# A relational graph layer: when a finished node tile is weighted, and in how many steps the next layer's front follows

## The chip, the core and the metric

The kernel runs on one core of one Trainium2 chip. Its time is the device time of one execution in microseconds (us); lower is better. TensorE (PE in the profile, with its weight loads as PEld) multiplies, VectorE (DVE) and ScalarE (ACT) do elementwise work and copies, GpSimd (POOL) issues gathers by software, and SyncE (SP) issues plain transfers. Each engine takes its instructions in program order.

## The reference

The model is a stack of four layers on a graph of 3125 nodes with 256 features and 50,000 edges. Each layer is a graph part and a feed-forward part, both added to the node features `x`. The change lies in the last layer's graph part, and in what opens the feed-forward part behind it:

```python
def _L3_gnn_ref(node_repr, weight, bias, edge_index, edge_types):
    h_all = jnp.einsum('ni,roi->rno', node_repr, weight)      # 8 relations
    src, dst = (edge_index[0], edge_index[1])
    msgs = h_all[edge_types, src]
    messages = jax.ops.segment_sum(msgs, dst, num_segments=node_repr.shape[0])
    return messages + bias

x = x + _L3_gnn_ref(_layernorm(x), ...)
x = x + _L3_ffn_ref(_layernorm(x), ...)   # 8 experts, the best one of each node, softmax(x @ gate_w + gate_b)
```

Each edge has one of 8 types (relations). A node receives the sum, over its incoming edges, of the source's normalised features times the matrix of the edge's type. The feed-forward part normalises `x` again, computes logits of 8 experts per node, and sends each node through its best expert, of limited capacity.

## The kernel before

The graph part sums first and multiplies afterwards: for every node and every relation the source features are summed over the edges of that type, and only the sums are multiplied by the relation's matrix. Edges are sorted by destination by an earlier stage. `l3_gnn` walks over them in 196 **quarters** of 256 edges, 16 destination nodes to a quarter on average; a node tile of 128 nodes is 8 quarters. One turn of the loop, quarter q:

- Two gathers by POOL (line 681), each of 128 edges' source rows, into the tile `g`. The rows are bf16 and hold three parts of 256 whose sum is the fp32 value, so a gather brings 196 KB. `g` has 12 buffers, one to a quarter.
- Two one-hot matrices `hot` on DVE (line 1703): 128 edges by 192 places (8 relations x 24 nodes).
- 12 bf16 matmuls on PE (line 1708): transposed features times one-hot into the PSUM tile `sum`, which has 4 buffers.
- DVE reads the quarter's place in the ring (line 1712) and adds `sum` to the running sums `acc` (line 1714). `acc` is a ring of 512 nodes plus a margin of 24.
- `weighted(1, q)`: one relation of the oldest tile that was taken out at least two quarters ago: two fp32 matmuls, which the trace shows as 4 rows (line 1685), from the copy `done` into the PSUM tile `po`.
- When the tile's last quarter has passed (`last[t] == q`), `finished(t)`: ACT copies the tile's sums to `done` (line 1664, two buffers) and clears them in `acc` (line 1665); for every fourth tile, where the ring wraps, the margin is added and cleared as well (lines 1669 and 1670).

After the eighth relation DVE adds `po` to `x` (line 1689), and `then` is called: `l3_ffn_front(t)`. It makes the layer norm of the tile (lines 529 to 534, on DVE with a square root on ACT), issues three transfers of 128 KB on SP (lines 1733, 1734 and 1737: the normalised tile, `x` for later, and `x` as the output so far), transposes the normalised tile on PE (two matmuls, `f_tr`, line 1740), copies that out of PSUM on ACT (`f_xT`, line 1742), multiplies by the gate's weights on PE (`f_mm`, line 563), and adds the gate's bias on DVE (`pr`, line 1745). `po` has two PSUM buffers, `f_tr` and `f_mm` one each.

The order of an engine's work is settled ahead of the run by a scheduler, from the order of the program and its estimates; waits between engines are semaphores. `tc.issue_after(i)` holds what is issued inside it behind instruction i on the engine of i. Before the change PE's order at the end of a tile is: a po row of the next tile's first relation, the two f_tr, the other po row, one sum of the next quarter, the two f_mm, the remaining eleven sums (rows here are matmuls as the program has them, two to a relation). For 185 sums no po comes at all; then one relation comes with each quarter. After the last sums 36 po rows follow, with the f_tr and f_mm of three tiles between and behind them.

The stage behind, `l3_ffn`, begins with the softmax of the logits on DVE and the experts' weight transfers on SP (line 1804), directly after this stage's end.

A second version of the graph part (`l3_gnn_of_any`) stands in the other branch of a test on the data; it does not run here.

Of the kernel before, what the change touches and what calls it, by code (L numbers as in the profile page):

```python
# [22 lines left out]
P = 128  # L23
# [4 lines left out]
D = 256  # L28
# [24 lines left out]
NQ = -(-E // QE)  # L53
# [10 lines left out]
def rows_of(t):  # L64
    return P if t < NT - 1 else TAIL
# [3 lines left out]
def gnn_ffn_stack(ctx: ExitStack, tc: tile.TileContext, a: dict, out: bass.AP):  # L69

    nc = tc.nc
# [890 lines left out]
    with ExitStack() as s:  # L962
        pp = s.enter_context(tc.tile_pool(reuse_waits="tile", name="l0_ps", bufs=2, space=PSUM))
# [3 lines left out]
        wp = s.enter_context(tc.tile_pool(reuse_waits="tile", name="l0f_w", bufs=2))  # L967
# [29 lines left out]
    with ExitStack() as s:  # L997
        sp = s.enter_context(tc.tile_pool(reuse_waits="tile", name="cells_s", bufs=1))
        bp = s.enter_context(tc.tile_pool(reuse_waits="tile", name="cells_x", bufs=2))
        pp = s.enter_context(tc.tile_pool(reuse_waits="tile", name="cells_ps", bufs=2, space=PSUM))  # L1000
# [132 lines left out]
    with tc.If(nc.values_load(slow_path[0:1, 0:1], min_val=0, max_val=1) > 0) as any_order:  # L1133
        with ExitStack() as s:
            ep = s.enter_context(tc.tile_pool(reuse_waits="tile", name="any_e", bufs=1))
            gp = s.enter_context(tc.tile_pool(reuse_waits="tile", name="any_w", bufs=3))
            pp = s.enter_context(tc.tile_pool(reuse_waits="tile", name="any_ps", bufs=2, space=PSUM))
            adj1 = build_graph_of_any(ep, gp, pp)
        with ExitStack() as s:
            lp = s.enter_context(tc.tile_pool(reuse_waits="tile", name="l1a", bufs=1))  # L1140
            wp = s.enter_context(tc.tile_pool(reuse_waits="tile", name="l1a_w", bufs=2))
            ap = s.enter_context(tc.tile_pool(reuse_waits="tile", name="l1a_adj", bufs=1))
            pp = s.enter_context(tc.tile_pool(reuse_waits="tile", name="l1a_ps", bufs=1, space=PSUM))
            l1_gnn_of_any(lp, wp, ap, pp, adj1)
    with any_order.Else():
        with ExitStack() as s:
            lp = s.enter_context(tc.tile_pool(reuse_waits="tile", name="l1g", bufs=1))
            wp = s.enter_context(tc.tile_pool(reuse_waits="tile", name="l1g_w", bufs=3))
            pp = s.enter_context(tc.tile_pool(reuse_waits="tile", name="l1g_ps", bufs=2, space=PSUM))
# [170 lines left out]
    with ExitStack() as s:  # L1320
        pp = s.enter_context(tc.tile_pool(reuse_waits="tile", name="l1f_ps", bufs=2, space=PSUM))
# [107 lines left out]
    with ExitStack() as s:  # L1429
        lp = s.enter_context(tc.tile_pool(reuse_waits="tile", name="l2g", bufs=1))  # L1430
        wp = s.enter_context(tc.tile_pool(reuse_waits="tile", name="l2g_w", bufs=2))
        ap = s.enter_context(tc.tile_pool(reuse_waits="tile", name="l2g_adj", bufs=3))
        pp = s.enter_context(tc.tile_pool(reuse_waits="tile", name="l2g_ps", bufs=2, space=PSUM))
# [180 lines left out]
    def l3_gnn_of_any(lp, wp, pp, wT, then):  # L1614

        rel = dram.tile([NP * NR, D], F32, name="rel")
        acc = lp.tile([P, NT, D], F32, name="acc")
        nc.vector.memset(acc, 0.0)
        xT = lp.tile([P, KC, NP], F32, name="xT")
        for t in range(0, NT, SG):  # L1620
            parts = wp.tile([P, SG, 3 * D], BF16, name="l3_in")
            nc.sync.dma_start(parts, tab_3[t * P : (t + SG) * P, :].rearrange("(t p) c -> p t c", p=P))
            z = wp.tile([P, SG, D], F32, name="l3_z")
            nc.vector.tensor_add(z, parts[:, :, :D], parts[:, :, D : 2 * D])
            nc.vector.tensor_add(z, z, parts[:, :, 2 * D :])
            for j in range(SG):
                ps = pp.tile([P, KC, P], F32, name="tr")
                for k in range(KC):
                    nc.tensor.transpose(ps[:, k, :], z[:, j, k * P : (k + 1) * P], ident)
                evict(xT[:, :, (t + j) * P : (t + j + 1) * P], ps)  # L1630
        rel_t = rel[:, :].rearrange("(n r) d -> n (r d)", r=NR)
        for t in range(NT):
            row = wp.tile([P, NR, D], F32, name="row")
            for r in range(0, NR, 2):
                ps = pp.tile([P, 2, D], F32, name="mm")
                by_node(ps, xT, t, wT[:, :, r : r + 2, :])
                evict(row[:, r : r + 2, :], ps)
            nc.sync.dma_start(rel_t[t * P : (t + 1) * P, :], row.rearrange("p r d -> p (r d)"))
        scattered_messages(acc, rel, pp)
        for g in range(0, NT, SG):  # L1640
            nc.vector.tensor_add(x[:, g : g + SG, :], x[:, g : g + SG, :], acc[:, g : g + SG, :])
            for t in range(g, g + SG):
                then(wp, pp, t)

    def l3_gnn(lp, wp, xp, pp, wT, then):


        NC = NR * DW
        iota_n = lp.tile([P, NC], BF16, name="iota_n")
        wide = lp.tile([P, NC], F32, name="iota_w")  # L1650
        nc.gpsimd.iota(wide, pattern=[[1, NC]], base=0, channel_multiplier=0, allow_small_or_imprecise_dtypes=True)  # L1651
        nc.vector.tensor_copy(iota_n, wide)
        zero = lp.tile([P, P], F32, name="zero")
        nc.vector.memset(zero, 0.0)

        acc = lp.tile([P, KC, NR, RING + DW], F32, name="acc")
        nc.vector.memset(acc, 0.0)

        def finished(t):

            c = t * P % RING
            done = wp.tile([P, KC, NR, P], F32, name="done")
            here = acc[:, :, :, c : c + P].rearrange("p k r n -> p (k r) n")
            nc.scalar.copy(done.rearrange("p k r n -> p (k r) n"), here)  # L1664
            nc.scalar.copy(here, zero[:, None, :].to_broadcast([P, KC * NR, P]))
            if c == 0 and t:
                over = acc[:, :, :, RING:].rearrange("p k r n -> p (k r) n")
                to = done[:, :, :, :DW].rearrange("p k r n -> p (k r) n")
                nc.vector.tensor_add(to, to, over)
                nc.scalar.copy(over, zero[:, None, :DW].to_broadcast([P, KC * NR, DW]))  # L1670
            return done


        last = [min((t + 1) * P // QN + SLACK // QN - 1, NQ - 1) for t in range(NT)]
        last[NT - 2] = END_Q - 1
        todo = []

        def weighted(n, q):

            while n and todo and todo[0][4] + 2 <= q:  # L1680
                t, done, po, r, _ = todo[0]
                if po is None:
                    po = todo[0][2] = pp.tile([P, D], F32, name="po")
                for k in range(KC):
                    nc.tensor.matmul(po, done[:, k, r, :], wT[:, k, r, :], start=(r == 0 and k == 0),  # L1685
                                     stop=(r == NR - 1 and k == KC - 1))
                todo[0][3] += 1
                if r == NR - 1:
                    nc.vector.tensor_add(x[:, t, :], po, x[:, t, :])
                    todo.pop(0)  # L1690
                    then(wp, pp, t)
                n -= 1

        t = 0
        added = []
        for q in range(NQ):
            g, s = q // 4, q % 4
            nt = min(PT, -(-(E - q * QE) // P))
            e = xp.tile([P, PT, 3 * D], BF16, name="g", bufs=12)
            hot = xp.tile([P, PT, NC], BF16, name="hot")  # L1700
            for j in range(nt):
                gather(e[:, j, :], tab_3[:, :], grp_src[:, s * PT + j, g : g + 1])
                nc.vector.tensor_scalar(hot[:, j, :], iota_n, grp_loc[:, s * PT + j, g : g + 1], None, op0=ALU.is_equal)  # L1703
            ps = pp.tile([P, KC, NC], F32, name="sum", bufs=4)
            for k in range(KC):
                for j in range(nt):
                    for i in range(3):
                        nc.tensor.matmul(ps[:, k, :], e[:, j, i * D + k * P : i * D + (k + 1) * P], hot[:, j, :],  # L1708
                                         start=(j == 0 and i == 0), stop=(j == nt - 1 and i == 2))

            with tc.issue_after(added[q - 3].ins) if q > 2 else nullcontext():
                at = nc.vector.value_load(grp_at[0:1, s, g : g + 1], min_val=0, max_val=RING - 1)
            to = acc[:, :, :, bass.ds(at, DW)]
            added.append(nc.vector.tensor_add(to, to, ps.rearrange("p k (r n) -> p k r n", r=NR)))  # L1714
            weighted(1, q)
            while t < NT and last[t] == q:
                todo.append([t, finished(t), None, 0, q])
                t += 1
        weighted(NR * NT, 2 * NQ)


    tab_x3 = dram.tile([NP, D], F32, name="tab_x3")
# [7 lines left out]
    def l3_ffn_front(wp, pp, t):  # L1730
        n = wp.tile([P, 1, D], F32, name="f_x")
        layer_norm(n, x[:, t : t + 1, :], 0, 1)
        nc.sync.dma_start(tab_x3[t * P : (t + 1) * P, :], n[:, 0, :])
        nc.sync.dma_start(raw_x3[t * P : (t + 1) * P, :], x[:, t, :])

        r = rows_of(t)
        nc.sync.dma_start(out[t * P : t * P + r, :], x[:r, t, :])
        pt = pp.tile([P, KC, P], F32, name="f_tr", bufs=1)
        for k in range(KC):
            nc.tensor.transpose(pt[:, k, :], n[:, 0, k * P : (k + 1) * P], ident)  # L1740
        xT = wp.tile([P, KC, P], F32, name="f_xT")
        nc.scalar.copy(xT, pt)
        ps = pp.tile([P, NE3], F32, name="f_mm", bufs=1)
        by_node(ps, xT, 0, gw_3)
        nc.vector.tensor_add(pr_3[:, t, :], ps, gb_3)
# [4 lines left out]
    with ExitStack() as s:  # L1750
        lp = s.enter_context(tc.tile_pool(reuse_waits="tile", name="l2f", bufs=1))
        wp = s.enter_context(tc.tile_pool(reuse_waits="tile", name="l2f_w", bufs=2))
# [223 lines left out]
```

## Time and profile before

| | us |
|---|---|
| three runs | 3268.21, 3270.93, 3270.08 |
| median of the runs | 3270.08 |
| the profiled execution | 3264.51 |
| its span, first to last instruction | 3262.6 |
| first gathers of the changed stage to its last `pr` | 2421 to 3057 |
| gathers of the stage, behind the first fill | 2472 to 3013 |
| PE busy over the span (PEld, DVE, ACT, POOL) | 83% (62%, 43%, 27%, 19%) |
| mean granted TensorE clock | 0.905 of full speed |

The profile shows one execution of its own, 5.6 us under the median of the timed runs. Times in it are microseconds from the first instruction. A line of the timeline gives start, duration, engine, line, operation, tiles (written <- read), shapes, and how many instructions it stands for; in brackets are the idle time of that engine ahead of it and what ended it ("issue" is idle time in which nothing that the profile shows was waited for, "remote" a semaphore whose sender it does not name). Waits are listed as engine, line and releaser with the total, the number, and the longest. Ends of matmuls are modelled, their starts recorded.

### The profile page before, as it was taken

Reading aid. Unit: us, or ns where it says so; the run is one execution under the profiler, and the core shown is the slowest. Engines: PE = TensorE matmul, PEld = TensorE weight load, DVE = VectorE, ACT = ScalarE, POOL = GpSimd, SP = SyncE. Lnnn points to the kernel's source line nnn. Section 1 sums busy time; section 2 is a strip of 40 time slices with the busy share of each in tenths; the row PEclk is TensorE's granted clock in tenths of the full one; section 3 lists DMA queues with packets and bytes.
Section 4 is the critical chain, followed back from the end, with each engine's and each line's share of the span. In section 5 each row is a group of like instructions: output and inputs, shape, how many; then the busy total and the mean of one; then the engine's idle time right before and its main releaser. Section 6 shows DMA issues by size and latency. Waiting matters only on the chain. (4 is left out here: it accounts for less than half of the span.)

```text
span 3262.6 us, 41054 instructions
## 1 busy us (share of the span) xinstructions
PE 2693.3 (83%) x14727; PEld 2034.3 (62%) x14727; DVE 1408.6 (43%) x3870; ACT 871.3 (27%) x2259; POOL 632.8 (19%) x660
## 2 busy tenths in 40 slices
PE   4488877778999869994799999998965878878688
PEld 3255766654775556553588888885433666666555
DVE  5764888863452362223812111114342333343422
ACT  1373488871220012332200000002320121121223
POOL 2600000000000001113200000000026666665132
PEclk9797999999999859997899999998986888888799
DMA  4200232230000343335243333321014555555542
GB/s 128 53 8 1 65 137 123 122 136 4 1 1 1 129 133 86 82 83 166 73 152 142 134 141 141 133 97 47 30 54 139 145 147 152 147 148 142 208 116 51
DMA packets 160019, 326.08 MB, mean 100 GB/s; under 512 B 44757, under 2 KB 116997, under 8 KB 150186
## 3 DMA queue, kind: packets, MB, share of 16 engines
q1 hardware_dynamic: 118005, 211.51, 19.3%
q0 software_dynamic: 37472, 108.23, 11.8%
q10 hardware_dynamic: 4308, 3.40, 0.4%
q8 instruction: 126, 2.06, 0.3%
q14 instruction: 108, 0.88, 0.1%
HBM read 244.26 MB, written 79.46 MB: 99 GB/s over the span
## 5 line engine op out<-in xcount | busy, mean ns | idle before, releaser
L1420 PE MATMUL agg<-h,adj 128*128 128x256 f32 x2500 | 545.7, 379 | 0.5 <-DVE h L1378 0.4
L1420 PEld LDWEIGHTS agg<-h,adj 128*128 128x128 f32 x2500 | 473.9, 190 | 65.3 <-DVE h L1378 1.5
L681 POOL DMA_INDIRECT g<-tab,grp_src x391 | 379.6, 971 | 228.4 <-issue 90.8
L1081 PE MATMUL agg<-hs,cnt 128*128 128x384 bf16 (+1 forms) x2500 | 335.4, 288 | 16.1 <-DVE s L1084 10.7
L1708 PE MATMUL sum<-hot,g 128*128 128x192 bf16 x2346 | 273.9, 268 | 83.1 <-issue 46.6
L1708 PEld LDWEIGHTS <-g 128*128 128x128 bf16 x2346 | 225.4, 108 | 135.5 <-issue 83.3
L1685 PE MATMUL po<-wT,done 128*128 128x256 f32 x800 | 249.8, 435 | 48.0 <-ACT done L1664 25.5
L1081 PEld LDWEIGHTS <-cnt 128*128 128x128 fp8e4 x2500 | 229.8, 100 | 94.9 <-issue 20.5
L324 PE MATMUL cell_w<-rows,wgt 128*128 128x125 f32 x1280 | 208.1, 301 | 78.0 <-ACT wgt L318 78.0
L324 PEld LDWEIGHTS cell_w<-rows,wgt 128*128 128x128 f32 x1280 | 168.6, 191 | 113.1 <-ACT wgt L318 88.7
L1714 DVE TENSOR_TENSOR acc<-acc,sum 128x384 f32 x196 | 108.1, 552 | 289.1 <-remote 120.7
L1422 DVE SCALAR_TENSOR_TENSOR o<-agg,dinv,b 128x256 f32<-128x256 f32 x50 | 24.2, 484 | 437.6 <-PE agg L1420 437.6
L318 ACT ACTIVATE wgt<-one,win_w 128x128 f32<-128x128 bf16 x480 | 208.0, 520 | 4.3 <-DVE one L312 3.4
L1685 PEld LDWEIGHTS po<-wT,done 128*128 128x128 f32 x800 | 154.7, 217 | 69.4 <-ACT done L1664 29.0
L1664 ACT COPY done<-acc 128x2048 f32<-128x2048 f32 x25 | 47.5, 1899 | 416.0 <-issue 370.8
L1651 POOL IOTA iota_w<- 128x192 f32 x1 | 0.3, 302 | 805.3 <-PE mm L1485 805.3
L1268 PE MATMUL mm<-w,xgT 128*128 x240 | 122.5, 616 | 10.5 <-ACT xgT L1264 10.5
L681 POOL DMA_INDIRECT xg<-tab_x,owner_l x76 | 71.9, 947 | 299.3 <-PE tr L1262 210.1
L1281 PE MATMUL po<-w,hT 128*128 x480 | 118.4, 389 | 11.3 <-ACT hT L1277 11.2
L309 DVE TENSOR_TENSOR rows<-iota_f,win_m 128x1000 f32<-128x1000 f32 x80 | 96.0, 1200 | 52.1 <-PE cell_w L324 50.8
L1703 DVE TENSOR_SCALAR hot<-iota_n,grp_loc 128x192 bf16<-128x192 bf16 x391 | 89.1, 286 | 64.0 <-issue 27.0
L1281 PEld LDWEIGHTS po<-w,hT 128*128 128x128 f32 x480 | 86.7, 189 | 46.0 <-ACT hT L1277 35.9
(544 smaller groups left out, 3866.7 us busy)
## 6 DMA issues: line engine op xcount, KB each, us to landing
adj<-adjw SPq DMA_DIRECT2D x50, 1600.0 KB
adjw<-cells_w SPq DMA_DIRECT2D x25, 1600.0 KB
w<-in_L_ffn_w_dram SPq DMA_DIRECT2D x16, 1024.0 KB
b<-in_L_ffn_b_dram SPq DMA_DIRECT2D x76, 128.0 KB
yb<-yo SPq DMA_DIRECT2D x76, 128.0 KB
w<-in_L_ffn_w_dram SPq DMA_DIRECT2D x16, 512.0 KB
w<-in_L_ffn_w_dram SPq DMA_DIRECT2D x32, 256.0 KB
g<-tab,grp_src POOLq DMA_INDIRECT x391
```

The lines of the kernel that those rows point to most:

```text
L309: nc.vector.tensor_tensor(rows, iota_f[:, None, : GN * NT].to_broadcast([P, WB, GN * NT]), win_m[:, q, None].to_broadcast([P, WB, GN * NT] ...
L318: nc.scalar.mul(wgt[:, i, :], one[:, :, i], win_w[:, g + i : g + i + 1])
L324: nc.tensor.matmul(pw[:, i // HB, c], wgt[:, i, :], rows[:, i, :], start=True, stop=True)
L681: nc.gpsimd.indirect_dma_start(out=dst, out_offset=None, in_=table, in_offset=bass.IndirectOffsetOnAxis(ap=idx, axis=0))
L1081: nc.tensor.matmul(ps[:, : 3 * m], cnt[:, k, t * P : (t + 1) * P], hs[:, k, : 3 * m], start=(k == 0), stop=(k == NT - 1))
L1268: nc.tensor.matmul(ph, xgT[:, k, :], w1[:, bass.ds(e, 1), k, :].rearrange("p e f -> p (e f)"), start=(k == 0), stop=(k == KC - 1))
L1281: nc.tensor.matmul(po, hT[:, f, :], w2[:, bass.ds(e, 1), f, :].rearrange("p e d -> p (e d)"), start=(f == 0), stop=(f == FC - 1))
L1420: nc.tensor.matmul(acc, ch[:, k, :], h[i][:, k, :], start=(k == 0), stop=(k == NT - 1))
L1685: nc.tensor.matmul(po, done[:, k, r, :], wT[:, k, r, :], start=(r == 0 and k == 0), stop=(r == NR - 1 and k == KC - 1))
L1703: nc.vector.tensor_scalar(hot[:, j, :], iota_n, grp_loc[:, s * PT + j, g : g + 1], None, op0=ALU.is_equal)
L1708: nc.tensor.matmul(ps[:, k, :], e[:, j, i * D + k * P : i * D + (k + 1) * P], hot[:, j, :], start=(j == 0 and i == 0), stop=(j == nt - 1 a ...
L1714: added.append(nc.vector.tensor_add(to, to, ps.rearrange("p k (r n) -> p k r n", r=NR)))
```

## The change

Three things change in `l3_gnn` and its `then`. First, a tile is weighted from the fourth quarter after its taking out, no longer from the second; from quarter 188 on it is the second still. Second, `l3_ffn_front` becomes a generator with two yields, so that it runs in three steps: the norm with its transfers; the transposes and their copy; the logits. After the eighth relation it is only put on a list, and `step()` advances each listed front by one step per quarter. Third, both `step()` and `weighted(1, q)` are held behind the last of the quarter's sums on PE. After the last quarter all that is left is weighted, and then the fronts are stepped to their ends.

PE's order becomes: twelve sums, two f_tr, two po, twelve sums, two f_mm, two po, twelve sums, and so on. The first po comes behind 192 sums. After the last sums 40 po rows stand in one piece; behind them four f_tr, four f_mm, two f_tr and two f_mm. The instructions are the same in kind and number.

```diff
-                then(wp, pp, t)
+                for _ in then(wp, pp, t):
+                    pass
...
+        steps = []
+        def lag(q):
+            return 4 if q < NQ - 8 else 2
+        def step():
+            for g in list(steps):
+                if next(g, None) is None:
+                    steps.remove(g)
         def weighted(n, q):
-            while n and todo and todo[0][4] + 2 <= q:
+            while n and todo and todo[0][4] + lag(q) <= q:
...
                     nc.vector.tensor_add(x[:, t, :], po, x[:, t, :])
                     todo.pop(0)
-                    then(wp, pp, t)
+                    steps.append(then(wp, pp, t))
...
-                        nc.tensor.matmul(ps[:, k, :], e[:, j, i * D + k * P : i * D + (k + 1) * P], hot[:, j, :],
+                        mm = nc.tensor.matmul(ps[:, k, :], e[:, j, i * D + k * P : i * D + (k + 1) * P], hot[:, j, :],
...
-            weighted(1, q)
+            with tc.issue_after(mm.ins):
+                step()
+                weighted(1, q)
...
         weighted(NR * NT, 2 * NQ)
+        while steps:
+            step()
...
         nc.sync.dma_start(out[t * P : t * P + r, :], x[:r, t, :])
+        yield 1
         pt = pp.tile([P, KC, P], F32, name="f_tr", bufs=1)
...
         nc.scalar.copy(xT, pt)
+        yield 1
         ps = pp.tile([P, NE3], F32, name="f_mm", bufs=1)
```

More of the change, by code (lines that the diff above doesn't have):

```diff
@@ L1707, in l3_gnn @@
                     for i in range(3):
-                        nc.tensor.matmul(ps[:, k, :], e[:, j, i * D + k * P : i * D + (k + 1) * P], hot[:, j, :],
-                                         start=(j == 0 and i == 0), stop=(j == nt - 1 and i == 2))
+                        mm = nc.tensor.matmul(ps[:, k, :], e[:, j, i * D + k * P : i * D + (k + 1) * P], hot[:, j, :],
+                                              start=(j == 0 and i == 0), stop=(j == nt - 1 and i == 2))
             with tc.issue_after(added[q - 3].ins) if q > 2 else nullcontext():
```

## Prediction

> **What bounds the kernel now.** I read the page first: the changed stage is the last graph layer, from about 2432 us (its iota, then the first gathers) to 3057 us. The order of views was then the waits of PE and of POOL, the stretches by window, and the timeline of one tile. The waits of PE between 2500 and 3000 us (total us, times, longest) name just what the change addresses:
>
> ```profile
> PE po L1685 <- ACT done L1664: 23.6, 13, 2.0
> PE f_mm L563 <- ACT f_xT L1742: 14.6, 14, 2.2
> ```
>
> That is 38 us of 500. The waits of POOL between 2472 and 3014 us say something else:
>
> ```profile
> POOL g L681 <- issue: 82.6, 271, 0.3
> POOL g L681 <- PE sum L1708: 51.5, 42, 1.9
> POOL g L681 <- remote: 45.4, 32, 5.2
> POOL g L681 <- PE f_tr L1740: 18.8, 11, 1.8
> ```
>
> POOL issues gathers back to back (0.95 us and 0.30 of "issue": 1.25 each, 16 to a tile, 20.0 us) and stops about three times a tile for a buffer of `g` that PE must free. Three windows (length, then busy us and count of PE, PEld, DVE, ACT, POOL, then clock, DMA share, GB/s):
>
> ```profile
> 2472.14:2495.75 23.61, 12.88 (x80) 10.03 (x77) 7.04 (x20) 0.00 (x0) 15.14 (x16) 0.57 0.48 133
> 2720.43:2744.37 23.94, 19.43 (x134) 16.09 (x134) 9.69 (x31) 4.37 (x5) 15.13 (x16) 0.86 0.53 149
> 3013.50:3035.40 21.90, 21.90 (x188) 19.51 (x187) 9.51 (x28) 8.17 (x6) 0.09 (x1) 1.00 0.09 28
> ```
>
> The first holds 16 gathers, eight quarters, before any tile is finished: sums only, no po, no copy of done, no front. The second is a whole tile (8 quarters, 8 relations, one taking out, one front). A full tile's work more costs 0.33 us. The third comes after the last gather: PE there goes on at 1.88 us a quarter (sum group at 2724.83, next at 2726.71: the same pace), and at that stretch's tile end the copy of done at 3020.93 and the front at 3026.25 make no gap. So what the tile end costs shows only while POOL issues. In the timeline of a tile (start, us; in brackets the idle time before and its releaser):
>
> ```profile
> 2728.59 1.15 PE L1708 MATMUL sum<-hot,g 128*128 128x192 bf16 x12
> ...
> 2735.14 0.56 DVE L1714 TENSOR_TENSOR acc<-acc,sum 128x384 f32 x1 [4.64 <-remote]
> 2735.38 0.94 POOL L681 DMA_INDIRECT g<-tab,grp_src  x1 [1.75 <-remote]
> 2735.73 1.90 ACT L1664 COPY done<-acc 128x2048 f32<-128x2048 f32 x1 [15.10 <-issue]
> 2737.68 2.08 PE L1685 MATMUL po<-wT,done 128*128 128x256 f32 x4 [2.00 <-ACT done L1664]
> 2742.38 0.64 PE L1740 MATMUL f_tr<-ident,f_x 128*128 128x128 f32 x2
> 2744.37 0.94 POOL L681 DMA_INDIRECT g<-tab,grp_src  x1 [1.80 <-PE f_tr L1740]
> 2744.62 0.61 PE L563 MATMUL f_mm<-gw,f_xT 128*128 128x8 f32 x4 [0.83 <-ACT f_xT L1742]
> ```
>
> The sums recorded as ending at 2729.74 let `acc` go only at 2735.14, 5.4 us later, 1.5 us after POOL's last gather (2732.69 + 0.95). Then acc, POOL and done start within 0.6 us. Releases of PE come late while POOL is busy, and arrive when POOL has stopped. The stops grow with the run before them:
>
> ```profile
> 2472.14 0.94 POOL L681 DMA_INDIRECT g<-tab,grp_src  x1 [5.17 <-remote]
> 2483.93 0.94 POOL L681 DMA_INDIRECT g<-tab,grp_src  x1 [2.10 <-remote]
> 2495.75 0.94 POOL L681 DMA_INDIRECT g<-tab,grp_src  x1 [2.10 <-remote]
> ```
>
> Idle time after runs of 2, 3, 4 and 15 quarters is about 1.35, 1.76, 2.10 and 5.17 us, so a quarter costs 2.50 + (idle - 0.30)/run: 3.03, 2.99, 2.95 and 2.82 us. Today's tile has runs of 3, 3 and 2: 23.94/8 = 2.99. I read that as the bound: POOL's chain of gathers and stops, with PE (15.0 us for eight quarters at full pace) below it.
>
> The Trainium skill speaks to the late release in "Perfetto Trace Analysis", section "Tensor Engine Instruction (MATMUL, LD_WEIGHTS)": the recorded end of a matmul is an estimate, and the semaphore goes out only after PSUM has acknowledged the write. The trace fits that the record is early, but 5.4 us is more than the page explains.
>
> **The change, part by part.** *Kinds and numbers of instructions* stay: 800 po and 2346 sums in the page's groups, 25 copies of done, 25 fronts with three 128 KB transfers on SP each. Nothing is added but an order on PE, which costs no instruction.
>
> *Lag four instead of two.* A tile's first relation comes behind the sums of quarter +4. Those reuse one of four `sum` buffers, so they already wait for the acc that done waits for; done takes 1.90 us, the sums 1.15, so at most 0.75 us of the 2.00 stays. What waits behind that po on PE is the next quarter's sums. This removes 1.25 to 2.0 us of PE standing per tile. What it is worth lies between nothing (POOL's chain is late anyway) and all of it (2.0 x 22.6 tiles in 541 us of gathers = 45 us).
>
> *Three steps.* Today f_mm follows f_tr with only two po rows and one sum between; PE stands 0.83 us there, and at worst 2.2. After it a whole quarter lies between (12 sums and 4 po rows, 1.88 us), while from f_tr's recorded end (2743.02) to the end of f_xT (2744.56) 1.54 us passed. So this wait goes if the release comes as here; worth 0 to 0.83 x 22.6 = 19 us. The transfers on SP stay with the norm, one quarter at most from their place, and SP has nothing else in this stage; POOL's queue holds only gathers, nothing is moved past them. DVE's pr and ACT's f_xT come a quarter later; no buffer turns on them (f_tr and f_mm have one each and come every eight quarters).
>
> *What is late next* is the `sum` buffer: PE cannot run more than four quarters past the last acc. In the first window, where nothing else stood in its way, that gave runs of exactly four. So I price the two edits together by run length. No change in runs: 0. Runs of four throughout: (23.61 - 23.94) x 22.6 = -7.5 us. Since f_tr and f_mm still stand between, at +4 and +5 quarters, each wanting a release, I take halfway, runs of three and four: (2.99 + 2.95)/2 x 8 = 23.76 us, -0.18 x 22.6 = **-4 us**. The cover of the rest is POOL's gathers; without it the standing itself would count (rival one).
>
> One rule speaks for far more. "TensorE: Matmul & The Clock Gate", section "HAM oscillation — how this bites in real kernels": idle stretches over some 3 us drop the clock to half. Here the granted clock is 0.50 for 6.83 us of each tile (2736.59 to 2743.41). By the rule, with the waits gone, 3.4 us a tile or 77 us would come back; by POOL's row the slow stretch is paid inside a stop that stays. The first window ran at 0.57 and was the fastest, so I go by the row.
>
> *The tail.* With lag 2 from quarter 188, the last three tiles become due as before, but tile 22 (due from 187) starts at 191 instead of 189: 19 relations instead of 17 are left after the loop. A tile of eight there took 3045.80 to 3053.67, 0.98 us a relation: +2.0 us. Two fronts' f_tr and f_mm (2 x (0.41 + 0.51) = 1.8 us) move from between the relations to behind them, where PE today stands 2.26 us for the last norm:
>
> ```profile
> 3055.43 0.41 PE L1740 MATMUL f_tr<-ident,f_x 128*128 128x128 f32 x2 [2.26 <-DVE f_x L534]
> 3056.36 0.61 PE L563 MATMUL f_mm<-gw,f_xT 128*128 128x8 f32 x4 [0.52 <-ACT f_xT L1742]
> ```
>
> They need a round by ACT between (about 0.9 us), so some 0.8 us pushes past that cover: 2.0 - 1.8 + 0.8 = **+1 us**; bounds 0 (all covered) and +3.2 (none covered, two pr on DVE ahead of the last). The expert weights' transfers start right behind (SP at 3056.43), so the tail counts whole.
>
> Sum: -4 + 1 = -3 us on the profiled execution's 3264.51 (span 3262.6, 1.9 us around it), 3261.5; the median shown is 5.6 us above that execution, so **3267**.
>
> **Rivals.**
> *One, PE is the bound.* For it: PE's own waits, 2.0 and 0.83 us a tile, and the half clock. Against: the first window, as slow with none of them. With PE no longer late, POOL would run at its floor, 20.0 us a tile: -3.94 x 22.6 = -89, to 3182 us. Chance 0.10.
>
> *Two, much longer runs.* acc at 2729.36 shows that some releases pass 3 us into a run. If PE never stands, buffers might come free during runs. Between 2.10 at four and 5.17 at fifteen, a run of six stops for about 2.7 us and one of twelve for 4.3: 2.89 and 2.84 us a quarter, -0.8 and -1.2 us a tile, -18 and -28 us, so 3253 to 3244. Against: four `sum` buffers. Chance 0.22.
>
> *Three, slower: a new stop for f_mm.* f_tr and f_mm now lie in two quarters, so one tile end may need two late releases instead of one. It decides when f_tr's release takes longer than the 1.88 us to f_mm; in order, the next sums stand behind f_mm, and POOL's runs break to 3, 2, 2 and 1 (stop of 1.17): 20.0 + 1.76 + 1.35 + 1.35 + 1.17 - 1.2 = 24.43, +0.49 x 22.6 = +11, with a tail of up to +3: 3281 to 3284. Chance 0.20.
>
> *The change moves the waits but not the time* is my forecast, as it were: the two rows of PE vanish, POOL's pace stays.
>
> **How the numbers follow.** Forecast 0.48, its own range 3263 to 3276 (-7 to +6 us: about the 0.2%, 6.5 us, that a measurement can tell from no change). Faster by more: rivals one and two, 0.32. Slower: 0.20. The range leaves out rival one and the outer ends of the others: 3240 to 3285.
>
> **What would show it.** Right: in the changed trace, po's wait for done is under 0.8 us, f_mm's for f_xT gone, POOL's stops two or three a tile after runs of three and four, 23.6 to 23.9 us from tile to tile. Wrong: gathers at 1.25 us through a whole tile (rival one), stops after six or more quarters (two), or a stop at each f_mm (three). A stage end later by over 3 us with an unchanged pace would say that I mis-sized the tail.

## The result, and the profile after

The changed kernel took 3281.45 us (median of 20 runs) and the kernel before, in the same runs, 3269.66 us. The ratio is 1.0038, 95% interval 1.0026 to 1.0050: the change costs 12 us. The interval leaves out 1, and the forecast had the other direction. The predicted time was 3267, the range 3240 to 3285.

The profiled executions differ by 9.8 us (span 3272.4 against 3262.6). Counted to the stage's last `pr`, the changed one is 11.1 us later: its first gather is 1.4 us earlier; from the 31st gather to the last (the *stretch* below: 22.6 tiles) it takes 548.8 us instead of 540.5; from the last gather to the end of the last sum 25.7 instead of 23.0; and from there to the end of the last `pr` 23.0 instead of 21.5. So +8.3, +2.7 and +1.4.

PE's waits between 2500 and 3000 us (total, times, longest), the answer to the two lines with which the prediction began:

```profile
PE f_tr L1760 <- DVE f_x L534: 55.4, 11, 6.5
PE f_tr L1760 <- issue: 27.3, 9, 3.4
...
PE f_mm L563 <- ACT f_xT L1762: 2.7, 1, 2.7
```

The wait of po for done is gone from the list and f_mm's is 2.7 us in all, as the change means it. In their place stand 82.7 us at f_tr (before, 5.9), all of them for the normalised tile: in each of the twenty, those called "issue" too, f_tr starts 0.06 us after the norm's last instruction has ended. POOL's waits between 2472 and 3014 us:

```profile
POOL g L681 <- issue: 80.7, 263, 0.6
POOL g L681 <- PE sum L1722: 72.2, 55, 2.9
POOL g L681 <- remote: 40.6, 26, 2.1
POOL g L681 <- PE f_mm L563: 8.5, 5, 1.8
```

Waits for sums went from 51.5 to 72.2 us, and the longest from 1.9 to 2.9. Tiles are no longer alike: before, 16 gathers took 23.6 to 24.3 us in every tile but the last (25.0); now, behind a first tile of 22.2, they take anything from 23.6 to 26.3. A slow one and a quick one (columns as before):

```profile
2618.44:2644.59 26.15, 20.15 (x134) 17.47 (x133) 9.45 (x32) 4.15 (x5) 15.14 (x17) 0.80 0.49 136
2728.67:2752.14 23.47, 18.66 (x138) 15.83 (x137) 10.00 (x34) 4.83 (x5) 15.14 (x16) 0.86 0.53 150
```

The timeline shows what happens in the slow one:

```profile
2624.22 0.42 DVE L1703 TENSOR_TENSOR x<-po,x 128x256 f32<-128x256 f32 x1 [0.89 <-PE sum L1722]
...
2624.91 0.43 DVE L529 BATCH_NORM_STATS2 ln_st<-x 128x6 f32<-128x256 f32 x1 [0.26 <-DVE x L1703]
...
2627.15 0.56 DVE L1728 TENSOR_TENSOR acc<-acc,sum 128x384 f32 x1 [1.81 <-remote]
2627.39 0.96 POOL L681 DMA_INDIRECT g<-tab,grp_src  x1 [1.75 <-remote]
2627.62 0.18 DVE L530 BATCH_NORM_AGGREGATE ln_mv<-ln_st 128x2 f32<-128x6 f32 x1
...
2629.04 0.41 DVE L534 TENSOR_SCALAR f_x<-x,ln_mv,ln_rs 128x256 f32<-128x256 f32 x1
...
2629.51 0.69 PE L1760 MATMUL f_tr<-ident,f_x 128*128 128x128 f32 x2 [6.00 <-DVE f_x L534]
...
2631.70 2.13 PE L1722 MATMUL sum<-hot,g 128*128 128x192 bf16 x12
...
2634.10 0.94 POOL L681 DMA_INDIRECT g<-tab,grp_src  x1 [2.00 <-PE sum L1722]
...
2638.63 0.94 POOL L681 DMA_INDIRECT g<-tab,grp_src  x1 [2.34 <-PE sum L1722]
```

DVE has begun the norm at 2624.91, but the next instruction in its order is an acc that waits for a late release; the norm's second half stands behind it until 2627.62 and ends at 2629.45. PE comes to f_tr at 2623.5 and stands 6.00 us, with the next quarter's sums behind f_tr. Then it works at half pace: 12 sums in 2.13 us instead of 1.15. POOL, which has resumed meanwhile, runs out of free buffers after four gathers and again after two, and now its stops (2.00 and 2.34 us) are not for a release that is late but for sums that PE has not done.

That gives a count. Before, the 69 stops of the stretch grow with the run before them (medians 1.13, 1.35, 1.75 and 2.10 us after two, four, six and eight gathers), and none after four gathers or fewer is over 1.6 us. After, ten of 79 are, 21.7 us together. Their excess over those medians is some 9 us, against 8.3 that the stretch grew. Such stops are called *long* below.

One thing in the part above has to be set right. In PE's order before the change, the po rows around f_tr belong to the next tile's second relation, not its first. So f_tr stands behind the tile's last relation by 24 sums and one whole relation, before and after alike (half a relation more before).

### The profile page after: what moved, and what is told of

Read it like the earlier page. It is cut to its first block, busy times and chain, and to the rows that moved or that the text cites. A ratio compares the mean times of both kernels' runs of the same rounds, so it can differ in the third digit from the quotient of the medians.

```text
span 3272.4 us, 41040 instructions
## 1 busy us (share of the span) xinstructions
PE 2677.2 (82%) x14727; PEld 2032.1 (62%) x14727; DVE 1408.2 (43%) x3870; ACT 873.1 (27%) x2259; POOL 631.5 (19%) x660
## 5 line engine op out<-in xcount | busy, mean ns | idle before, releaser
L1722 PE MATMUL sum<-hot,g 128*128 128x192 bf16 x2346 | 266.9, 266 | 87.3 <-issue 51.5
L1699 PE MATMUL po<-wT,done 128*128 128x256 f32 x800 | 235.0, 423 | 3.7 <-issue 3.3
L309 DVE TENSOR_TENSOR rows<-iota_f,win_m 128x1000 f32<-128x1000 f32 x80 | 96.0, 1200 | 51.9 <-PE cell_w L324 50.6
```

Of the source, the lines that this page charges most:

```text
L309: nc.vector.tensor_tensor(rows, iota_f[:, None, : GN * NT].to_broadcast([P, WB, GN * NT]), win_m[:, q, None].to_broadcast([P, WB, GN * NT] ...
L1722: mm = nc.tensor.matmul(ps[:, k, :], e[:, j, i * D + k * P : i * D + (k + 1) * P], hot[:, j, :], start=(j == 0 and i == 0), stop=(j == nt ...
```

## The experiments

The kernels of a group ran beside the kernel before on one chip, most with 11 or 12 runs to its 21 to 35 (c_lag has 6, c_before one). The groups are of two kinds. In the second, third and fifth, before took 3253 to 3266 us and PE's releases came late, as in the first pair (the engine that waits goes on microseconds after the recorded end of PE's work). In the first and fourth it took 3129 and 3130 us, and releases were prompt. What sets the two kinds apart the record does not show; it names chip 3 for a group of each kind.

**First group: the parts, where releases are not late.**

The lag alone (in the kernel before), the steps alone, the changed kernel with one more quarter ahead of f_tr, and with another tail:

```diff
e1_lag, in the kernel before:
-            while n and todo and todo[0][4] + 2 <= q:
+            while n and todo and todo[0][4] + (4 if q < NQ - 8 else 2) <= q:
e2_steps, in the changed kernel:
-            return 4 if q < NQ - 8 else 2
+            return 2
e3_norm_wait, in the changed kernel, behind the norm's transfers:
         yield 1
+        yield 1
e6_tail, in the changed kernel:
-        weighted(NR * NT, 2 * NQ)
-        while steps:
-            step()
+        while todo or steps:
+            step()
+            weighted(1, 2 * NQ)
```

> The lag alone: before, with four quarters in place of two (two from quarter 188), the front as before, its transposes two quarters behind the tile's last relation. Theory (the loss is f_tr, which the steps put one quarter nearer to the last relation, ahead of its norm): the wait of po for done falls under 0.8 us a time, f_tr waits little, the gathers' stretch (31st to last gather) is at most 541 us as before, the time 0.997 to 1.001 of before. Rival A (the lag itself breaks the rhythm): stretch 546 us or more, 1.002 to 1.005. Rival B (the order behind the sums): like the theory. Rival C (the tail): +2 us in the tail only, 1.000 to 1.001.

> The steps alone: the changed kernel with a lag of two throughout. Theory: f_tr stands near the last relation, and po's wait for done of 2.0 us is back, which gives the norm time: the stretch of the gathers between 541 and 549 us, 1.000 to 1.004. Rival A (the lag): 540 us, 0.999 to 1.001. Rival B (the order behind the sums): 546 us or more, 1.002 to 1.005. Rival C (the tail): stretch 540 us, tail as in the changed kernel less 2 us.

> The changed kernel with one more quarter between the norm and the transposes (a second yield), so that f_tr comes two quarters behind the last relation, as before the change. Theory: f_tr's waits (83 us in 20 tiles of the changed kernel) fall under 20 us, the stretch of the gathers from 549 to at most 541 us, the time 8 to 13 us under the changed kernel, 0.997 to 1.001 of before. Rivals A and B: stretch stays at 546 us or more, 1.002 to 1.005. Rival C: 1.002 to 1.004, tail +1 us at most.

> The changed kernel with another tail: after the last quarter one step of the fronts and one relation in turn, in place of all relations and then the fronts. Theory: stretch of the gathers stays at 546 to 551 us; from the last gather to the last pr 46 to 47.5 us in place of 48.6; 1.003 on before, 1 to 2 us under the changed kernel. Rival C (the tail is the loss): last gather to the last pr 44.5 us or less, 1.000 to 1.001.

Measured: 0.9999 (0.9987 to 1.0012), 0.9994 (0.9981 to 1.0008), 1.0002 (0.9989 to 1.0016) and 1.0003 (0.9991 to 1.0015). All four missed what they were made for, since there was nothing to tell apart: the stretch is 451 us in each. One tile of the lag alone:

```profile
2699.94:2719.94 20.00, 16.46 (x136) 13.75 (x134) 9.52 (x30) 4.89 (x5) 15.14 (x16) 1.00 0.62 178
```

16 gathers in 20.00 us, the same POOL time of 15.14 as in the tiles of the first pair, a clock of 1.00, and not one stop in 360 gathers. PE now waits for gathered data (62.0 us, 81 times). So POOL's floor of 20.0 us, which the prediction worked out, is real. And POOL's being busy does not by itself make PE's releases late, as the prediction read it: here it is busier, and acc follows the recorded end of its sums by 0.04 us in the median of 109 waits, all but two of them within 0.5 us (2.6 us in the median in the profile of before).

**Second group: the same, with late releases.** Both kernels, the further quarter and the lag alone; the edits are as above.

> The changed kernel once more, on the chip of this call. The first four experiments ran on a chip where POOL never stops in this stage (16 gathers in 20.0 us in every tile) and where all four took the time of before. If this chip is of that kind: 20.0 us a tile, ratio 0.999 to 1.001, tail 1 to 3 us longer. If PE's releases come late here as in the first pair: 1.002 to 1.005, f_tr waits for f_x in half of the tiles, stretch of the gathers 545 us or more.

> The kernel before once more, for its trace on the chip of this call: a stretch of the gathers of 451 us without stops, or of 540 us with stops after runs of three, three and two quarters.

> The changed kernel with one more quarter between the norm and the transposes, on the chip of this call. With late releases: theory (f_tr stands one quarter too near behind the last relation) a stretch of at most 541 us, f_tr's waits under 20 us in all, 0.997 to 1.001; the rivals (lag, or the order behind the sums) 546 us or more, 1.002 to 1.005. Without late releases: 451 us, 0.999 to 1.001 by all theories.

> The lag alone, on the chip of this call. With late releases: theory a stretch of at most 541 us, 0.997 to 1.001; rival (the lag) 546 us or more, 1.002 to 1.005; rival (the order behind the sums) like the theory. Without late releases: 451 us, 0.999 to 1.001 by all theories.

| | ratio to before | stretch, us | long stops | last gather to last pr |
|---|---|---|---|---|
| c_before (one run) | | 534.3 | 1 | 45.1 |
| c_after | 1.0034 (1.0021 to 1.0046) | 542.0 | 7 | 49.4 |
| c_norm_wait | 0.9998 (0.9984 to 1.0011) | 532.5 | 1 | 44.0 |
| c_lag | 1.0064 (1.0049 to 1.0080) | 549.9 | 13 | 50.6 |

The single long stop of c_before and of c_norm_wait, and one of c_after's seven, comes before the first tile is finished and has nothing to do with f_tr.

The result repeats, though the stretch of c_after is under the 545 us that I gave. One more quarter ahead of f_tr takes all of it away, the longer tail included, even with 35 us of waits left at f_tr where I expected under 20. But the lag alone is the slowest of all, where my theory had at most 1.001. That theory said that the steps had moved f_tr nearer to the last relation. It falls: the lag alone has f_tr where all the others have it. Its waits of PE (2500 to 3000 us):

```profile
PE f_tr L1740 <- DVE f_x L534: 86.3, 15, 6.7
PE f_tr L1740 <- issue: 15.6, 4, 4.5
```

and in c_norm_wait:

```profile
PE f_tr L1761 <- DVE f_x L534: 16.7, 9, 5.2
PE f_tr L1761 <- issue: 15.7, 8, 3.4
```

What the lag takes away is po's wait for done. Before, that wait lay between the last relation and f_tr, and started at the same late release as the norm did; while PE stood at po (2.0 us in the tile shown ahead of the prediction, then the relation and 12 sums), the norm was made. The new theory: the wait on done was the cover of the norm.

**Third group: is it the lag?** The steps alone again, the steps at the old lag with the further quarter, two further quarters at the new lag, and five buffers of `sum`:

```diff
d_steps: as e2_steps.    d_old_lag: e2_steps and e3_norm_wait together.
d_norm_wait3, behind the norm's transfers:
         yield 1
+        yield 1
+        yield 1
d_five: e3_norm_wait, and
-            ps = pp.tile([P, KC, NC], F32, name="sum", bufs=4)
+            ps = pp.tile([P, KC, NC], F32, name="sum", bufs=5)
...
-        pt = pp.tile([P, KC, P], F32, name="f_tr", bufs=1)
+        both = pp.tile([P, KC * P + NE3], F32, name="f_tr", bufs=1)
+        pt = both[:, : KC * P].rearrange("p (k n) -> p k n", k=KC)
...
-        ps = pp.tile([P, NE3], F32, name="f_mm", bufs=1)
+        ps = both[:, KC * P :]
```

> The steps alone (lag of two throughout), asked again where releases come late. The lag alone was the slowest (1.0064), though PE's order has f_tr 24 sums behind the tile's last relation there, as before and as in the changed kernel; so the first theory, that the steps moved f_tr nearer, falls. New theory: what covered the norm was po's wait for done, between the last relation and f_tr; the lag takes it away, and PE now comes to f_tr ahead of the norm. Expected by it for the steps with the old lag: done's waits are back (0.5 to 1 us a tile), f_tr's waits stay under 35 us as in before, stretch 531 to 537 us where before has 534, 0.998 to 1.002. Rival (the steps and their order behind the sums cost something themselves): 539 us or more, 1.002 to 1.004. Without late releases: 451 us, 0.999 to 1.001 by both.

> The steps with one more quarter ahead of f_tr, and the old lag of two: done's wait and the further quarter both cover the norm. New theory: f_tr's waits go (under 10 us in all), stretch 529 to 535 us, 0.997 to 1.000, so that the lag of four is worth at most 0.1% in any place. Rival (the lag of four is worth something once f_tr is out of the way, as the change means it): at least 4 us slower than the lag of four with the same further quarter. Without late releases: 451 us, 0.999 to 1.001.

> The changed kernel with two more quarters between the norm and f_tr. New theory: f_tr's remaining waits (35 us with one more quarter) go to under 10 us; the gathers' pace is already set by POOL's stops, so the stretch falls by 0 to 3 us only, 0.997 to 1.000. If f_tr's waits were the pace: each 10 us of them gone takes up to 10 us off, 0.992 to 0.995. Without late releases: 451 us, 0.999 to 1.001.

> The changed kernel with one more quarter ahead of f_tr and five buffers of sum in place of four (f_tr and f_mm share one PSUM bank for it). If PE's way ahead of acc is what ends POOL's runs at four quarters, runs of five appear, at about 2.92 us a quarter in place of 2.95 to 2.99: stretch 524 to 531 us, 0.996 to 0.999. If the runs are ended by f_tr or f_mm, nothing changes: 532 us, 0.999 to 1.001. Without late releases: 451 us, 0.999 to 1.001.

| | ratio to before | stretch, us | long stops | last gather to last pr |
|---|---|---|---|---|
| d_steps | 0.9985 (0.9975 to 0.9995) | 540.2 | 2 | 41.9 |
| d_old_lag | 0.9996 (0.9984 to 1.0007) | 540.1 | 0 | 43.0 |
| d_norm_wait3 | 0.9998 (0.9987 to 1.0009) | 539.8 | 0 | 42.4 |
| d_five | 0.9987 (0.9975 to 0.9999) | 539.2 | 2 | 44.1 |

There is no trace of before from this group; its median of 3266 us is near the first pair's, where the stretch was 540.5. (The stretches that I gave for the steps alone, the old lag and the five buffers were counted from the 534 of c_before; they are missed by 3 to 8 us.) The steps alone are a little faster than before, so the loss is the lag's. The lag of four is worth nothing that can be measured even with f_tr out of the way (0.9998 with one further quarter and 0.9998 with two, against 0.9996 with one at the old lag; the intervals overlap). In d_norm_wait3 PE stands 6.8 us at f_tr in all, and it is no faster than c_norm_wait with its 35. Another expectation failed: the steps alone have more waits at f_tr than I allowed:

```profile
PE f_tr L1760 <- DVE f_x L534: 51.7, 14, 4.3
```

52 us of waits without a loss. So it is not the sum of PE's waits that costs (c_before has 36 us at f_tr, too, and no long stop from them); these did not lengthen POOL's stops. Why they do not can be read from the traces, though it was not tested apart. One tile of the steps alone:

```profile
2741.82 0.94 POOL L681 DMA_INDIRECT g<-tab,grp_src  x1 [1.74 <-remote]
2743.49 0.69 PE L1760 MATMUL f_tr<-ident,f_x 128*128 128x128 f32 x2 [4.24 <-DVE f_x L534]
2743.97 2.13 PE L1722 MATMUL sum<-hot,g 128*128 128x192 bf16 x12
2747.85 0.95 POOL L681 DMA_INDIRECT g<-tab,grp_src  x1 [1.33 <-PE f_mm L563]
```

Here the next quarter's sums follow f_tr directly and end 4.3 us after POOL has resumed, while POOL is still busy with four gathers (4.7 us). In the changed kernel a relation stands between, and the norm is later: in the slow tile above the sums end at 2633.83, 6.4 us after POOL resumed at 2627.39, and POOL goes on 0.27 us behind them. In the four tiles with a long stop after four gathers the sums end 6.2 to 6.4 us after POOL has resumed, in c_lag 6.3 to 7.1 (but for one stop there after three gathers).

Five buffers of `sum` did not bring runs of five quarters; runs of three and four stay. So the 0.9987, which is what I gave for runs of five, has another cause, which is open, or is chance.

**Fourth and fifth group: only the norm's lateness taken away.** The norm is put behind the tile's fifth relation in place of its eighth, and made from `x` without this layer's messages, so that it waits for no relation; f_tr, the lag and PE's order stay. Left out are the messages in the normalised tile, the logits and the choice of experts. Beside it, the steps at the old lag with five buffers of `sum` (without the further quarter):

```diff
f_early_norm, in the changed kernel:
+                if r == NR - 4:
+                    early[t] = then(wp, pp, t)
+                    next(early[t])
                 if r == NR - 1:
...
-                    steps.append(then(wp, pp, t))
+                    steps.append(early.pop(t))
...
         nc.sync.dma_start(tab_x3[t * P : (t + 1) * P, :], n[:, 0, :])
+        yield 1
```

> The changed kernel with the norm four relations earlier, of x without this layer's messages (so the normalised tile, the logits and the choice of experts leave the messages out), the rest in its place: f_tr stands where it does in the changed kernel, but its data are long ready. Theory (POOL's extra stops come from PE standing at f_tr for the norm, behind a late release): no stops over 1.6 us after four gathers or fewer (7 to 10 in the changed kernel), stretch within 3 us of before or under it, 0.996 to 1.000 of before. Rival (the later start of a tile's relations costs by itself, through done, po or the sums): 1.002 to 1.004, the long stops stay. Without late releases: 451 us, 0.999 to 1.001.

> The two edits that were under before, together: the steps with a lag of two, and five buffers of sum. Theory: neither meets the norm's wait; 0.997 to 0.999 of before, stretch 0 to 5 us under before's. Rival (they gain the same thing): no better than the steps alone, 0.998 to 1.000. Without late releases: 451 us, 0.998 to 1.000.

These two fell where releases are prompt: 0.9995 (0.9986 to 1.0004) and 0.9992 (0.9982 to 1.0003), stretch 451 us, no stops. That tells nothing of the question. Once more, with the changed kernel beside them:

> The changed kernel with the early norm once more (messages left out of the normalised tile, the logits and the choice of experts), since the last call's chip had no late releases. With late releases: theory no stops over 1.6 us after four gathers or fewer, at least 0.2% under the changed kernel on this chip, 0.996 to 1.000 of before; rival (the later start costs by itself) 1.002 to 1.004 with the long stops. Without: 0.999 to 1.001.

> The changed kernel on the same chip, for the comparison. With late releases: 1.002 to 1.005, 7 or more stops over 1.6 us after four gathers or fewer. Without: 20.0 us a tile, 0.999 to 1.001.

> The steps with a lag of two and five buffers of sum, once more. With late releases: 0.997 to 0.999 if the two gains add up, 0.998 to 1.000 if they are one gain. Without: 0.999 to 1.000.

| | ratio to before | stretch, us | long stops | last gather to last pr |
|---|---|---|---|---|
| g_after | 1.0036 (1.0023 to 1.0048) | 539.2 | 6 | 48.4 |
| g_early_norm | 0.9997 (0.9984 to 1.0011) | 531.8 | 1 | 42.9 |
| g_steps_five | 0.9992 (0.9981 to 1.0003) | 533.0 | 1 | 42.2 |

The lag is the same, and so is PE's order up to the last two fronts; only the norm stands elsewhere, and its result is ready 30 to 42 us ahead of f_tr in every tile but the first. The loss is gone, its stops (the one that is left comes before the first tile is finished) and the longer tail with it. The other choice of experts is not the reason: behind the last `pr` it takes 205.0 us, the changed kernel 205.2. PE's waits in g_early_norm:

```profile
PE sum L1726 <- issue: 44.9, 82, 1.2
PE f_mm L563 <- issue: 35.2, 12, 4.6
PE po L1700 <- issue: 12.0, 22, 0.9
```

There is no f_tr among them. PE stands at f_mm instead, 41 us for f_xT, and that lengthens no stop. This experiment moves the norm and leaves f_tr; c_norm_wait moves f_tr and leaves the norm, DVE's order included; both take the loss away. This is what I call shown: the lag costs because PE then stands at f_tr for the norm. The two small gains do not add up. With late releases, the only versions whose interval lies under 1 are the steps alone (0.9985) and, barely, five buffers with the further quarter (0.9987).

## Why the prediction was wrong

- **POOL's chain as the bound: right, with a wrong cause.** The pace did stay at 23.5 to 24 us in most tiles where nothing new got in, and where PE's waits at po or at f_tr went or moved without a long stop (c_norm_wait, d_norm_wait3, g_early_norm) the time is within 0.03% of before. That POOL's being busy is enough to make releases late is refuted by the groups with 20.0 us a tile; what else it takes is open.
- **"Lag four instead of two": the failed step.** I priced what the wait on done was worth between nothing and all of it (45 us), a gain in any case; for the norm that it covered I put down nothing. A wait that goes uncovers what was made behind it, and I named as late next only the `sum` buffers. The rows were in the timeline that I had read, though I did not show these two:

```profile
2736.55 0.42 DVE L1689 TENSOR_TENSOR x<-po,x 128x256 f32<-128x256 f32 x1
2740.26 0.44 DVE L534 TENSOR_SCALAR f_x<-x,ln_mv,ln_rs 128x256 f32<-128x256 f32 x1
```

Done was copied from 2735.73, `x` added from 2736.55, the norm ended at 2740.70, and f_tr came at 2742.38. Without the 2.00 us of standing and the half pace after it, PE would have been at f_tr before 2740.70 (2742.38 less 2.00 is 2740.38). What came of it: +8 us in the gathers and most of +4 behind them, instead of -4 and +1.
- **"Three steps": a gain inside the range, but not by the reason given.** f_mm's wait fell from 14.6 to 2.7 us (with "issue" from 17.9 to 3.9), yet only because PE had stood at f_tr before it. Where that stand is short or gone, f_mm waits for f_xT in spite of the quarter between: 11.6 us in the steps alone, 36.6 in d_norm_wait3, 40.8 in g_early_norm. I had made it a condition that f_tr's release comes as in the tile I read; often it comes later. The steps alone measure 0.9985, 5 us, inside the 0 to 19 that I gave.
- **The tail.** From the last sum to the last `pr` +1.4 us, predicted +1. But the stage's end behind the last gather grew by 4.1: 2.7 of it because PE is further behind when the gathers end. With the norm early the whole of it is shorter than before (42.9 against 45.1).
- **Rival three** had the right sign, the right size (3281 to 3284) and the broken runs, but the wrong place: it put the stop at f_mm, for f_tr's release. f_mm waits for almost nothing; f_tr waits for the norm. And where f_mm does wait (g_early_norm), it breaks no run. So the size agrees by luck, and so does the range: 3281.45 lies inside 3240 to 3285 only because the range took in this rival; the forecast's own 3263 to 3276 is missed.
- **The clock.** I weighed the rule of the Trainium skill ("TensorE: Matmul & The Clock Gate", section "HAM oscillation — how this bites in real kernels") against the first window and went by the window, which held for the kernel before. In the changed one the granted clock does matter, for after f_tr's 6.00 us there is no stop left to hide it:

```profile
2629.51:2638.40 8.89, 8.89 (x39) 7.62 (x40) 2.65 (x11) 0.37 (x1) 3.86 (x5) 0.50 0.49 138
2639.41:2644.59 5.18, 5.18 (x47) 4.76 (x46) 1.44 (x6) 3.37 (x2) 3.01 (x5) 1.00 0.52 138
```

PE is busy all through both windows, in the first at 0.50, while POOL waits for its sums twice. The rule, that idle stretches over some 3 us drop the clock to half, agrees with these rows. It does not cover the tile before the change: there 6.83 us ran at 0.50 behind idle stretches of at most 2.00 us. So the 77 us that the prediction worked out by the rule had no such stretch under them. How much of the loss is the half clock and how much the standing was not tested apart.

## What to carry to other kernels

Before a wait is removed, list what is made while the engine stands there, and look up when that is ready: the next instruction in order inherits the wait, and here the heir was longer. An engine in order pays for a chain on another engine at the first instruction that reads it, so put at least as much independent work ahead of that instruction as the chain takes, counted from its late release. And count the stops of the engine that sets the pace, not the sum of waits of another: 52 us of waits at f_tr cost nothing where they lengthened no stop, 83 cost 12 where they did.

## What the runs showed that was not expected

The same kernel takes 3129 us in some groups and 3253 to 3270 in others, and some 110 us of it lie in this stage (636 us in the first pair's before, 525 with the lag alone in the first group, whose time was that of before there): 451 us of gathers without a stop, against 532 to 550 with some 67 to 80 stops. POOL's instructions take the same 0.95 us in both. What differs is when PE's release reaches the other engines: nearly always within 0.5 us in the one, 5.4 us in the tile that the prediction reads in the other, while POOL issues gathers. What makes it the one or the other is open. The change costs 0.34 to 0.38% where releases are late; where they are prompt the changed kernel itself was not run, but its lag, its steps, and both with another tail or with a further quarter, all measure within 0.06% of before.
